# Three edits in a two-layer cross-attention kernel: seven block products for the FFN's down product, the fold of the sums of squares between the halves of the V projection, the index constants in a step of their own

## The chip, the cores and the metric

The kernel runs on one core of a Trainium2 chip. A core has a matrix engine (TensorE, PE in the profile, with its weight loads shown apart as PEld), a vector engine (VectorE, DVE), a scalar engine (ScalarE, ACT), a general engine (GpSimd, POOL) and a queue that issues the transfers (SyncE, SP). Each engine works through its own queue in order; semaphores tie the queues together. The metric is the device time of one execution in microseconds (us), as the median of several executions. Apart from these, one execution is recorded by the hardware profiler; the views of the profile are of that one.

## The reference: what is computed

2048 tokens of width 512 pass through four blocks, each with a residual: cross attention, a gated feed-forward network, a second cross attention, and a small memory network. In short:

```python
x = x + xattn0(layernorm(x), ctx)      # 32 query heads, 8 key/value heads of 128, rotary positions
w_gu = dequant(qweight_gu, qzeros_gu, scales_gu, g_idx_gu)      # 4-bit weights, 512 x 2752
gate, up = split(layernorm(x) @ w_gu)                           # 1376 columns each
w_d = dequant(qweight_down, qzeros_down, scales_down, g_idx_down)
x = x + (silu(gate) * up) @ w_d                                 # the down product, 1376 -> 512
q, k = rmsnorm(h @ wq, q_w), rmsnorm(ctx @ wk, k_w)             # second attention, h = layernorm(x)
x = x + (softmax(q @ k.T / sqrt(128) + mask) @ v) @ wo
x = x + memory_network(layernorm(x))
```

`dequant` is `scale[g] * (nibble(w) - (nibble(z)[g] + 1))`, where `g` is the group that an index list gives for each row. The rms norm of the second attention divides each head's vector by the root of its mean square, so it needs sums of squares over the 128 elements of a head.

## The kernel before

The tokens are worked on in four chunks of 512 (`c`). In an attention layer a step is one pair of a key/value head `g` (0 to 7) and a chunk `c` (0 to 3), 32 steps per layer. The feed-forward network has 24 steps: six groups of hidden columns (five of 256, the last of 96) by four chunks. Everything is 32-bit floating point; a matmul of the program shows as two instructions in the trace.

**Block products.** Most large products are done by a scheme that needs seven block products instead of eight for a product of 2 by 2 blocks. `left_sums` (L166 to L169, on POOL) forms four sums of the left operand's blocks, `right_sums` (L174 to L177, on POOL) four of the right operand's; a tile of seven blocks (`NBLK`) holds the four originals and the sums. `product` (L186) multiplies one pair of blocks, given by the table `PRODUCTS`, into one bank of PSUM, the memory that PE writes to. Two forms use it. `quarters` makes the four quarters of a result from seven products, for the query projection (P from xnT and wq) and for the gate and up product (P from xnT and wgu); ACT copies intermediate results out (h, L209). The attention's output product (O from oT and wo) adds its seven products into the residual `x_sb` with VectorE (L592): five adds cover one quarter (512 elements per partition), two cover a half (1024). Product 6 accumulates onto the bank of product 1 and product 7 onto that of product 6, each after the add that reads the bank.

**An attention step.** `run` writes the steps one after another, with the next step's projections amid the present step's work: the rest of the previous output product (4, 6, 5, 3, 7) with the pieces of the present softmax between, the next step's key projection (pk, L339) and query projection (P), the present step's product of probabilities and values (po, L566), which ACT copies to oT (L574), the next step's V projection (pv, L369), the first two output products, and the next step's scores (S, L470).

**The fold in the second attention.** VectorE reduces the squares of keys and queries to partial sums (kpart L357, part L425). `norms` adds them up across partitions with small matmuls against a constant (pm, L445 and L452), VectorE adds the epsilon (qs, L458), POOL raises the result to the power -1/2 (qr, L229 in `rsqrt`), and VectorE spreads the query factors over the partitions (rb, L278). The scores are multiplied by both factors (L504), POOL adds the mask (L514), VectorE takes maxima (r2x, L525). `run` calls `norms` for the next step after the values product, then `left_sums(oT)`, then the V projection.

**The feed-forward network.** A step makes hT = silu(gate) * up for one group and chunk (`ffn_up`; VectorE adds L878, POOL products L885). The down product of the previous step follows (`ffn_down`, L896): per 128 tokens two matmuls, 128 x 512, and one add into the residual (L903). In steps 1 to 3 of a group the next group's weights are unpacked (`nibbles`, L836) and dequantised (L831, L832), with small matmuls (pgz, pdz, L850) that gather scales and zero points by one-hot rows.

**The index constants.** `ffn_constants` is a generator: each of its pieces is emitted in one step of the first attention, from step (1,0) on, behind an add of the output product. The first piece makes the index columns pidx (L727 to L730) and also the first 512 columns of scales (casts L744 and L746, products L745). Later pieces take further scales, then zero points, then the one-hot rows.

A tile framework gives each engine its queue. Within what the program's order and the buffers allow, it chooses the order of instructions on each queue by their priorities, so an edit to the order of emission can shift instructions on several engines.

Of the kernel before, what the change touches and what calls it, by code (L numbers as in the profile page):

```python
# [44 lines left out]
def tile_xattn_ffn_2_layers(ctx: ExitStack, tc: tile.TileContext, a: dict, out: bass.AP):  # L45
# [133 lines left out]
    def product(which, ps, left, right, widths=(P, P), first=True):  # L179


        l, r = PRODUCTS[which]
        pv = ps.rearrange("p (m n) -> p m n", m=2)
        for m, w in enumerate(widths):
            for k in range(2):
                nc.tensor.matmul(  # L186
                    pv[0:w, m, :],
                    left[:, l, k, m * P : m * P + w],
                    right[:, r, k, :],
                    start=(first and m == 0 and k == 0),  # L190
                    stop=(k == 1),
                    skip_group_check=True,
                )

    def quarters(n, left, right, done, widths=(P, P)):


        size = (slice(0, widths[0]), slice(0, len(widths) * HC))

        def mul(which, ps=None):  # L200
            new = ps is None
            if new:
                ps = mm_tile(f"P{which}_{n}")
            product(which, ps, left, right, widths, first=new)
            return ps

        def copy(which, ps):
            t = half_tile(f"h{which}_{n}")
            nc.scalar.copy(t[size], ps[size])  # L209
            return t  # L210

        x = mul(1)
        p1 = copy(1, x)
        done(0, 0, p1, mul(2))
        mul(6, x)
        u2 = copy(2, x)
        w = mul(5)
        p5 = copy(5, w)
        mul(3, w)
        done(0, 1, u2, w)  # L220
        mul(7, x)
        u3 = copy(3, x)
        done(1, 1, p5, x)
        done(1, 0, u3, mul(4))


    def rsqrt(dst, src):
# [59 lines left out]
    class Attention:  # L287
# [71 lines left out]
            )  # L359
            return kT, part  # L360

        def project_v(self, g, c, ctxT):
            n = f"{self.L}_{g}_{c}"
            wkv = self.wkv[g]
            v = ap_.tile([P, TT, HD], F32, tag="v", name=f"v{n}")
            ps = mm_tile(f"pv{n}")
            for t in range(TT):
                for k in range(KT):
                    nc.tensor.matmul(  # L369
                        ps[:, t * HD : (t + 1) * HD],  # L370
                        ctxT[:, k, t * P : (t + 1) * P],
                        wkv[:, k, 1, :],
                        start=(k == 0),
                        stop=(k == KT - 1),
                    )
            nc.scalar.copy(v.rearrange("p t d -> p (t d)"), ps)
            return v
# [205 lines left out]
            return ps  # L583

        def out_add(self, c, rows, cols, ps, over=None):

            x = x_sb[c].rearrange("p (i t) (j w) -> p i t j w", i=2, j=2)
            dst = x[:, rows] if cols is None else x[:, :, :, cols] if rows is None else x[:, rows, :, cols]
            src = ps.rearrange("p (t w) -> p t w", t=2)
            if over is not None:  # L590
                src = src.unsqueeze(over).to_broadcast(dst.shape)
            self.added = nc.vector.tensor_tensor(dst, dst, src, ALU.add).ins  # L592

        def output_first(self, g, c, oT):

# [39 lines left out]
        def run(self, hooks, joined, after, between=lambda c: None, tail=lambda: None, late={}):  # L635
# [15 lines left out]
            for i, (g, c) in enumerate(steps):  # L651
                more = i + 1 < len(steps)
                if c == NCH - 1 and g + 1 < NKV:
                    self.load_kv(g + 1)
                for hook in hooks.get((g, c), ()):
                    hook()
                ctx_next = ctx_of(i + 2) if i + 2 < len(steps) else None
                if g == NKV - 1 and c > 1:
                    between(c - 2)
                pieces = self.softmax(g, c, st, scales)  # L660

                def middle():
                    if c == NCH - 1 and g + 1 < NKV:
                        with tc.issue_after(self.pooled):
                            left_sums(self.wq[g + 1])

                if before is not None:
                    probs = self.output_rest(*before, pieces, middle)
                    with tc.issue_after(self.added):
                        for hook in late.get((g, c), ()):  # L670
                            hook()
                else:
                    *_, probs = pieces
                if c == 0 and g > 0:
                    self.load_out(g)
                done = before is not None and before[0] == NKV - 1
                if done:
                    joined(before[1])
                if more:
                    kT, kpart = self.project_k(*steps[i + 1], ctxT)  # L680
                    if c == 0:
                        right_sums(self.wo[g])
                    qT, part = self.project_q(*steps[i + 1])
                    if c == NCH - 2 and g + 1 < NKV:
                        self.load_q(g + 1)
                else:
                    tail()
                if done:
                    after(before[1])
                oT = self.values(g, c, v, probs)  # L690
                if more:
                    scales = self.norms(*steps[i + 1], kpart, part)
                self.pooled = left_sums(oT)
                if more:
                    v = self.project_v(*steps[i + 1], ctxT)
                before = self.output_first(g, c, oT)
                if more:
                    st = self.scores(*steps[i + 1], kT, qT)
                ctxT = ctx_next
# [10 lines left out]
    def ffn_constants():  # L710
# [5 lines left out]
        for base, cnt, parts in ((R_GS, NG, 3), (R_GZ, NG, 1), (R_DS, NGD, 3), (R_DZ, NGD, 1)):  # L716
# [11 lines left out]
            nc.vector.tensor_scalar(p2, idx, float(2 * cnt), -1.0, ALU.is_ge, ALU.mult)  # L728
            for p_ in (p1, p2):
                nc.vector.scalar_tensor_tensor(idx, p_, float(cnt), idx, ALU.mult, ALU.add)  # L730
        for base, cnt, name in ((R_GS, NG, "scales_gu"), (R_DS, NGD, "scales_down")):
            rows = slice(base, base + 3 * cnt)
            _, p1, p2 = (pidx[rows, k : k + 1] for k in range(3))
# [33 lines left out]
        for base, cnt, parts, name in (  # L767
# [7 lines left out]
            for at in range(0, total, CH):  # L775
# [11 lines left out]
                    oh[rows, at : at + w], o, pidx[rows, 0:1], None, ALU.is_equal  # L787
                )
                yield
        ffn["sz"], ffn["oh"] = sz, oh  # L790

    groups = [(f, min(FG, INTER - f)) for f in range(0, INTER, FG)]
    wgu, wd = {}, {}
# [17 lines left out]

    def ffn_load_down(i):

        d = (
            q_tile(f"wd{i}")[:, 0:2]
            if i % 2 == 0
            else o_tile(f"wd{i}").rearrange("p b h w -> p b (h w)")[:, 0:2]
        )
        for t, (f, w_) in enumerate(ffn_tiles(i)):
            nc.sync.dma_start(  # L820
                d[0:w_, t, :].bitcast(U32),
                a["qweight_down"][f // 8 : (f + w_) // 8, :]
                .unsqueeze(1)
                .to_broadcast([w_ // 8, 8, D]),
            )
        wd[i] = d

# [12 lines left out]
    def ffn_dequant(i, what=None):  # L840
# [18 lines left out]
        if what in (None, 1):  # L859
            left_sums(w, fw)  # L860
        for t, (f, w_) in enumerate(ffn_tiles(i)) if what in (None, 2) else ():
            nibbles(d[0:w_, t, :], w_)
            pp = [mm_tile(f"pdz{i}_{t}_{side}") for side in range(2)]
            for side, rows in enumerate((slice(R_DS, R_DS + 3 * NGD), slice(R_DZ, R_DZ + NGD))):
                nc.tensor.matmul(
                    pp[side][0:w_, :], oh[rows, f : f + w_], sz[rows, 0:D], start=True, stop=True
                )
            dequant(d[0:w_, t, :], pp[0][0:w_, :], pp[1][0:w_, :])

    def ffn_up(i, c):  # L870
        hT = tmp_tile(f"hT{i}_{c}")
        widths = [w_ for _, w_ in ffn_tiles(i)]
        size = (slice(0, widths[0]), slice(0, len(widths) * HC))

        def quarter(j, half, x, y):

            x, y = x[size], y[size]
            nc.vector.tensor_tensor(x, x, y, ALU.add)  # L878
            h = hT[0 : widths[0], 0 : len(widths), half * HC : (half + 1) * HC]
            xv = x.rearrange("p (t w) -> p t w", w=HC)  # L880
            if j == 0:
                nc.scalar.activation(xv, xv, AF.Silu)
                held[half] = xv
            else:
                nc.gpsimd.tensor_tensor(h, held[half], xv, ALU.mult)  # L885

        held = {}
        quarters(f"{i}_{c}", wgu[i], xnT[c], quarter, widths)
        return hT

    def ffn_down(i, c, hT):
        tiles = ffn_tiles(i)
        for tk in range(TT):
            p = mm_tile(f"pd{i}_{c}_{tk}")
            for t, (f, w_) in enumerate(tiles):
                nc.tensor.matmul(  # L896
                    p,
                    hT[0:w_, t, tk * P : (tk + 1) * P],
                    wd[i][0:w_, t, :],
                    start=(t == 0),  # L900
                    stop=(t == len(tiles) - 1),
                )
            nc.vector.tensor_tensor(x_sb[c][:, tk, :], x_sb[c][:, tk, :], p, ALU.add)  # L903

    def ffn_run(hooks, joined, last):
# [398 lines left out]
```

## Time and profile before

| | us |
|---|---|
| median of 3 executions | 2937.34 (2937.07 to 2941.98) |
| the profiled execution | 2943.32 |
| its span in the profile | 2941.5 |
| first attention, about | 0 to 1206 |
| feed-forward network, about | 1206 to 1677 |
| second attention, about | 1677 to 2860 |
| memory network, to the end | 2860 to 2941.5 |

| engine, busy us | first attention | feed-forward | second attention | end |
|---|---|---|---|---|
| PE | 1155.9 | 470.2 | 1156.1 | 56.7 |
| DVE | 884.4 | 200.0 | 677.2 | 50.5 |
| ACT | 399.4 | 94.5 | 303.1 | 23.2 |
| POOL | 624.9 | 114.4 | 523.9 | 20.7 |

The mean granted clock of PE over the execution was 0.987 of full speed. A row of a timeline reads: start, duration, engine, line, operation, out<-in, shape, number of instructions merged into the row, and in square brackets the idle time before it with what ended it. A row of the waits reads: who waited <- for whom: us in total, times, the longest one. A row of the groups reads: line, engine, operation, out<-in, shapes, count | busy us, mean ns of one | idle time before, releaser.

### The profile page before, as it was taken

Reading aid. Unit: us, or ns where it says so; the run is one execution under the profiler, and the core shown is the slowest. Engines: PE = TensorE matmul, PEld = TensorE weight load, DVE = VectorE, ACT = ScalarE, POOL = GpSimd, SP = SyncE. Lnnn points to the kernel's source line nnn. Section 1 sums busy time; section 2 is a strip of 40 time slices with the busy share of each in tenths; the row PEclk is TensorE's granted clock in tenths of the full one; section 3 lists DMA queues with packets and bytes.
Section 4 is the critical chain, followed back from the end, with each engine's and each line's share of the span. In section 5 each row is a group of like instructions: output and inputs, shape, how many; then the busy total and the mean of one; then the engine's idle time right before and its main releaser. Section 6 shows DMA issues by size and latency. Waiting matters only on the chain.

```text
span 2941.5 us, 40415 instructions
## 1 busy us (share of the span) xinstructions
PE 2838.8 (97%) x16502; PEld 2217.1 (75%) x16502; DVE 1812.1 (62%) x2752; ACT 820.2 (28%) x1397; POOL 1283.9 (44%) x932
## 2 busy tenths in 40 slices
PE   7999999999999999899999999999999999999987
PEld 5878787778887787676666677777777777787765
DVE  7667777777777766544433665555555555555565
ACT  3323333333333333211111222222222222222232
POOL 5544545454545455411222444444445353535432
PEclk9999999999999999899999999999999999999998
DMA  4111111111111111000000102120202020201001
GB/s 159 40 44 44 52 45 51 49 60 51 45 52 44 51 44 58 23 22 22 20 8 17 36 29 67 34 65 30 65 29 65 30 65 29 65 31 64 15 1 58
DMA packets 103807, 130.71 MB, mean 44 GB/s; under 512 B 8725, under 2 KB 65165, under 8 KB 103623
## 3 DMA queue, kind: packets, MB, share of 16 engines
q1 hardware_dynamic: 103047, 127.09, 13.3%
q8 instruction: 130, 2.13, 0.3%
q10 hardware_dynamic: 576, 1.05, 0.1%
q14 instruction: 54, 0.44, 0.1%
HBM read 123.92 MB, written 4.19 MB: 44 GB/s over the span
## 4 chain that ended last, share of the span: by engine, by line
PE 80%; DVE 12%; ACT 3%; issue 2%; POOL 2%; DMA 0%; DVEq 0%; ACTq 0%; POOLq 0%
PE P L186 30%; PE O L186 22%; PE pv L369 8%; PE pk L339 6%; PE pd L896 5%; PE S L470 4%; DVE part L425 2%; PE po L566 2%; DVE x L592 2%; DVE qT L419 1%; ACT q L421 1%; ACT rq L384 1%; DVE S L493 1%; PE pqy L1014 1%; DVE r2x L525 1%
## 5 line engine op out<-in xcount | busy, mean ns | idle before, releaser
L186 PE MATMUL P<-xnT,wq 128*128 128x256 f32 x3584 | 799.2, 382 | 23.4 <-ACT h L209 21.9
L186 PE MATMUL O<-wo,oT 128*128 128x256 f32 x3584 | 803.8, 382 | 4.2 <-ACT oT L574 3.3
L186 PEld LDWEIGHTS P<-xnT,wq 128*128 128x128 f32 x3584 | 678.8, 191 | 159.2 <-issue 39.2
L186 PEld LDWEIGHTS O<-wo,oT 128*128 128x128 f32 x3584 | 671.4, 190 | 118.0 <-issue 22.1
L592 DVE TENSOR_TENSOR x<-x,O 128x512 f32<-128x512 f32 (+1 forms) x448 | 368.5, 823 | 145.6 <-PE O L186 145.1
L546 POOL TENSOR_TENSOR s<-s,ib 128x512 f32<-128x512 f32 x128 | 169.6, 1347 | 489.0 <-DVE ib L278 480.5
L209 ACT COPY h<-P 128x512 f32<-128x512 f32 (+1 forms) x352 | 200.1, 573 | 365.4 <-PE P L186 354.5
L388 POOL TENSOR_TENSOR qT<-h,rq 128x512 f32<-128x512 f32 x128 | 175.4, 1370 | 277.1 <-DVE rq L387 267.2
L186 PE MATMUL P<-xnT,wgu 128*128 128x256 f32 (+1 forms) x1232 | 273.8, 382 | 0.0
L540 ACT ACTIVATE s<-s 128x1024 f32<-128x1024 f32 x64 | 67.7, 1057 | 708.1 <-DVE s L538 708.1
L186 PEld LDWEIGHTS P<-xnT,wgu 128*128 128x128 f32 (+1 forms) x1232 | 228.0, 187 | 47.1 <-issue 7.4
L229 POOL TENSOR_TENSOR qr<-qs,nhalf 128x20 f32<-128x20 f32 x32 | 113.4, 3543 | 335.0 <-DVE qs L458 335.0
L369 PE MATMUL pv<-wkv,ctxT 128*128 128x128 f32 x1984 | 238.0, 278 | 3.0 <-DVE h L401 1.7
L369 PEld LDWEIGHTS pv<-wkv,ctxT 128*128 128x128 f32 x1984 | 226.2, 192 | 14.0 <-issue 8.6
L384 ACT COPY rq<-h 64x512 f32<-64x512 f32 x256 | 157.9, 617 | 245.3 <-DVE h L401 242.9
L339 PE MATMUL pk<-ctxT,wkv 128*128 128x512 f32 x496 | 223.1, 592 | 0.0
L419 DVE TENSOR_TENSOR qT<-h,P 128x512 f32<-128x512 f32 x128 | 83.9, 674 | 170.4 <-PE P L186 170.4
L885 POOL TENSOR_TENSOR hT<-h,h 128x512 f32<-128x512 f32 (+1 forms) x48 | 55.6, 1179 | 283.4 <-DVE h L878 263.7
L339 PEld LDWEIGHTS pk<-ctxT,wkv 128*128 128x128 f32 x496 | 94.1, 190 | 92.9 <-issue 89.9
L896 PE MATMUL pd<-wd,hT 128*128 128x512 f32 (+1 forms) x352 | 155.0, 592 | 0.0
L386 DVE TENSOR_TENSOR h<-h,cosT 128x512 f32<-128x512 f32 x128 | 90.0, 703 | 105.0 <-ACT rq L384 105.0
L878 DVE TENSOR_TENSOR h<-h,P 128x512 f32<-128x512 f32 (+1 forms) x96 | 59.6, 640 | 151.9 <-PE P L186 103.7
(235 smaller groups left out, 3234.4 us busy)
## 6 DMA issues: line engine op xcount, KB each, us to landing
ctxT<-in_ctxT SPq DMA_DIRECT2D x62, 1024.0 KB
wq<-in_L_wq SPq DMA_DIRECT2D x32, 256.0 KB
wo<-in_L_wo SPq DMA_DIRECT2D x32, 256.0 KB
wq<-in_L_wqT SPq DMA_DIRECT2D x32, 256.0 KB
wo<-in_L_woT SPq DMA_DIRECT2D x32, 256.0 KB
wgu<-in_qweight_gu SPq DMA_DIRECT2D x40, 128.0 KB
out<-o SPq DMA_DIRECT2D x16, 256.0 KB
x<-in_x SPq DMA_DIRECT2D x12, 256.0 KB
```

The source lines that it names most:

```text
L186: nc.tensor.matmul(pv[0:w, m, :], left[:, l, k, m * P : m * P + w], right[:, r, k, :], start=(first and m == 0 and k == 0), stop=(k == 1), ...
L209: nc.scalar.copy(t[size], ps[size])
L229: nc.gpsimd.tensor_tensor(dst, src, nhalf[:, : src.shape[-1]], ALU.pow)
L339: nc.tensor.matmul(ps, wkv[:, k, 0, :], ctxT[:, k, :], start=(k == 0), stop=(k == KT - 1))
L369: nc.tensor.matmul(ps[:, t * HD : (t + 1) * HD], ctxT[:, k, t * P : (t + 1) * P], wkv[:, k, 1, :], start=(k == 0), stop=(k == KT - 1),)
L384: nc.scalar.copy(t[lo:hi, 1], src[HD - hi : HD - lo])
L388: nc.gpsimd.tensor_tensor(dst(None), dst(x), dst(t[:, 1]), ALU.add)
L419: nc.vector.tensor_tensor(q, xv, yv, ALU.add)
L470: nc.tensor.matmul(s5[j * KB : (j + 1) * KB, f, e], kT[:, f, e, j], qT[:, f * 4 + j].rearrange("p h q -> p (h q)"), start=True, stop=True,)
L546: nc.gpsimd.tensor_tensor(sv[:, f], sv[:, f], ib[:, f * W : (f + 1) * W].unsqueeze(1).to_broadcast([P, KH, W]), ALU.mult,)
L592: self.added = nc.vector.tensor_tensor(dst, dst, src, ALU.add).ins
L896: nc.tensor.matmul(p, hT[0:w_, t, tk * P : (tk + 1) * P], wd[i][0:w_, t, :], start=(t == 0), stop=(t == len(tiles) - 1),)
```

## The change

Three places change. First, in the five full groups the down product takes the scheme of seven block products: `right_sums` of the down weights after their dequantisation, `left_sums` of hT after its making, then seven products of two matmuls (four instructions) 128 x 256, whose results a new function `join` adds into the residual (the former body of `out_add`). hT and the down weights lie in tiles of seven blocks; for full groups hT takes a buffer of the context tiles. The last group of 96 keeps the old form. Second, `norms` is called between the two halves of the V projection, and `left_sums(oT)` is emitted after the V projection. Third, the index columns end with a `yield` of their own, so the first scales and all later pieces come one step later.

```diff
@@ product
-            for k in range(2):
+            for k in range(left.shape[2]):
...
-                    stop=(k == 1),
+                    stop=(k == left.shape[2] - 1),
@@ new function; out_add now calls it
+    def join(c, rows, cols, ps, over=None):
+
+        x = x_sb[c].rearrange("p (i t) (j w) -> p i t j w", i=2, j=2)
+        dst = x[:, rows] if cols is None else x[:, :, :, cols] if rows is None else x[:, rows, :, cols]
+        src = ps.rearrange("p (t w) -> p t w", t=2)
+        if over is not None:
+            src = src.unsqueeze(over).to_broadcast(dst.shape)
+        return nc.vector.tensor_tensor(dst, dst, src, ALU.add).ins
@@ project_v
-        def project_v(self, g, c, ctxT):
+        def project_v(self, g, c, ctxT, middle=lambda: None):
...
             for t in range(TT):
+                if t == TT // 2:
+                    middle()
                 for k in range(KT):
@@ run
                 oT = self.values(g, c, v, probs)
                 if more:
-                    scales = self.norms(*steps[i + 1], kpart, part)
+                    scales = []
+
+                    def middle():
+                        scales.append(self.norms(*steps[i + 1], kpart, part))
+
+                    v = self.project_v(*steps[i + 1], ctxT, middle)
+                    scales = scales[0]
                 self.pooled = left_sums(oT)
-                if more:
-                    v = self.project_v(*steps[i + 1], ctxT)
@@ ffn_constants
                 nc.vector.scalar_tensor_tensor(idx, p_, float(cnt), idx, ALU.mult, ALU.add)
+        ffn["sz"], ffn["oh"] = sz, oh
+        yield
         for base, cnt, name in ((R_GS, NG, "scales_gu"), (R_DS, NGD, "scales_down")):
...
-        ffn["sz"], ffn["oh"] = sz, oh
@@ ffn_load_down
+        d = home[:, 0 : NBLK * HC].rearrange("p (b k w) -> p b k w", b=NBLK, k=1)
@@ ffn_dequant
+        if what in (None, 2) and fw == FG:
+            right_sums(d)
@@ ffn_up
-        hT = tmp_tile(f"hT{i}_{c}")
+        if len(ffn_tiles(i)) == 2:
+            hT = ctx_tile(f"hT{i}_{c}").rearrange("p a b -> p (a b)")[:, 0 : NBLK * HC]
+        else:
+            hT = tmp_tile(f"hT{i}_{c}").rearrange("p a b -> p (a b)")
+        hT = hT.rearrange("p (b k w) -> p b k w", k=1, w=HC)
...
         quarters(f"{i}_{c}", wgu[i], xnT[c], quarter, widths)
+        if len(widths) == 2:
+            left_sums(hT)
@@ ffn_down
+        if len(tiles) == 2:
+
+            def mul(which, ps=None):
+                new = ps is None
+                if new:
+                    ps = mm_tile(f"D{which}_{i}_{c}")
+                product(which, ps, hT, wd[i], first=new)
+                return ps
+
+            x = mul(1)
+            join(c, 0, 0, x)
+            join(c, 0, 0, mul(2))
+            join(c, 1, 0, mul(4))
+            mul(6, x)
+            join(c, 0, 1, x)
+            join(c, None, 1, mul(5), 1)
+            join(c, 0, 1, mul(3))
+            mul(7, x)
+            join(c, 1, None, x, 2)
+            return
```

## The prediction

> **What bounds the kernel now.** I read the page first (busy shares, groups), then PE's waits, then the timeline of one step of each stage that the change touches.
>
> ```profile
> PE 2838.8 (97%) x16502; PEld 2217.1 (75%) x16502; DVE 1812.1 (62%) x2752; ACT 820.2 (28%) x1397; POOL 1283.9 (44%) x932
> L229 POOL TENSOR_TENSOR qr<-qs,nhalf 128x20 f32<-128x20 f32 x32 | 113.4, 3543 | 335.0 <-DVE qs L458 335.0
> L896 PE MATMUL pd<-wd,hT 128*128 128x512 f32 (+1 forms) x352 | 155.0, 592 | 0.0
> ```
>
> PE is busy for 97%: time is won by giving it less, or lost where it is made to stop. Of its waits, the part concerns these two:
>
> ```profile
> PE P L186 <- ACT h L209: 21.9, 15, 6.2
> PE pm L445 <- DVE part L425: 10.9, 29, 0.6
> ```
>
> The first holds the 6.2 us at the first step with index constants; the second is the fold of layer 1, 29 stops of 0.376. Now a feed-forward step and the gate/up product behind it (start, duration):
>
> ```profile
> 1303.84 7.03 PE L896 MATMUL pd<-wd,hT 128*128 128x512 f32 x16
> 1310.70 12.38 PE L186 MATMUL P<-xnT,wgu 128*128 128x256 f32 x56
> 1322.92 7.03 PE L896 MATMUL pd<-wd,hT 128*128 128x512 f32 x16
> ```
>
> From start to start: 6.86 us for 16 matmuls 512 wide, 0.429 each; 12.22 for 56 matmuls 256 wide, 0.218 each. And a step of layer 1, from the fold on:
>
> ```profile
> 2032.93 2.05 ACT L574 COPY oT<-po 128x512 f32<-128x512 f32 x4 [0.50 <-PE po L566]
> 2033.23 0.27 PE L445 MATMUL pm<-part,fold 128*32 128x16 f32 x7 [0.37 <-DVE part L425]
> ...
> 2033.91 3.54 POOL L229 TENSOR_TENSOR qr<-qs,nhalf 128x20 f32<-128x20 f32 x1 [12.11 <-DVE qs L458]
> 2037.16 3.62 PE L186 MATMUL O<-wo,oT 128*128 128x256 f32 x16
> ...
> 2037.42 1.27 POOL L166 TENSOR_TENSOR oT<-oT 128x512 f32<-128x512 f32 x1
> 2037.49 0.71 DVE L278 STREAM_TRANSPOSE rb<-qr 128x512 f32<-128x512 f32 x1 [3.66 <-POOL qr L229]
> 2039.10 0.69 DVE L592 TENSOR_TENSOR x<-x,O 128x512 f32<-128x512 f32 x1 [0.90 <-PE O L186]
> ...
> 2041.22 1.29 POOL L169 TENSOR_TENSOR oT<-oT 128x512 f32<-128x512 f32 x1
> 2042.58 8.90 PE L186 MATMUL O<-wo,oT 128*128 128x256 f32 x40
> ```
>
> PE runs fold, V projection, output products 1 and 2, scores, then 4, 6, 5, 3, 7, without a stop behind the fold. POOL's power (3.54 us) starts as soon as the fold is done, and its four left sums follow (5.09 from 2037.42 to the end of L169). DVE is in order: rb waits for the power, and the adds of products 1 and 2 stand behind rb.
>
> **Down product.** In 20 of 24 steps 16 matmuls of 0.429 (6.86) become 28 matmuls 256 wide. Price by the nearest rows: 0.2182 (the 56 above), 0.2185 (40 output products in 8.74, 2042.58 to 2051.32), upper bound 803.8/3584 = 0.224 (the group, with its slow stretches). At 0.2185: 6.12, so 0.74 a step, 14.8 in all (11.6 at 0.224).
> The Trainium skill, page "TensorE: Matmul & The Clock Gate", section "Back-to-back issue gap", speaks against this: sustained it gives about 81 ns at 128 columns and 131 at 512, so halving the width does not halve the time. An estimate from it, 98 ns at 256 by a straight line, makes 28 halves 1.31 times 16 wholes: 2.1 us lost per step, 42 in all. The two rows above disagree (0.218 against 0.429), and the measurement decides.
>
> Beside PE: DVE's 4 adds become 5 of 512 and 2 of 1024 elements, by the output products' adds (0.69 alone, 0.65 in a row, 1.21 for 1024). Laid behind the seven products of 0.875, from the first at 0: adds end at 1.76, 2.64, 3.52, 4.40, 5.80 (the double one), 6.5, 7.8. Product 7 needs the fourth at 5.25: it has it. The next matmuls take banks at 6.12 (of products 4, 2, 5: free by 5.8), 6.8 (needs 6.5) and 8.5 (needs 7.8): no stop. Only in the four steps c = 3 do three nibble operations of 0.49 (L836), which wait for weights, stand among these adds; the sixth then ends near 7.2, 0.5 late. That is 2 us in all, and up to 3 each, 12, if the weights are later. Should the adds fall behind in all 15 steps with dequantisation by 0.7, 11 are lost: that end stays for the range. Four left sums of hT (POOL, 1.27 each, one step ahead of their use) and four right sums per group lie under 18.4 us steps in which POOL works 114 of 471 us; without that cover a step would wait up to 5.1. hT now lives in context buffers, so two context loads of layer 1 go behind one set of its wq loads on SP's queue, 30 to 40 us before their use: nothing. **Down: -14.8 + 2 = -12.8** (-15 to 0).
>
> **Fold amid the V projection.** 31 of 32 folds move back by 8 of 16 matmuls, 1.84 us of PE (half of the 3.67 from 2033.49 to 2037.16). The stop of 0.376 goes, since the last partial sum (DVE, to 2033.17) is there: -10.9 in all, no more. What is late next? The power is now behind the four left sums in POOL's queue: in 31 steps the changed program issues L166 to L169 first, then L229, because the fold comes late while oT is ready with its last copy at 2034.98. From there, by these rows (times less 2000):
> left sums 35.06 to 40.15; power to 43.68 (before: 37.45); rb 43.72 to 44.43; add of product 1 to 45.01. PE, 0.37 earlier, ends product 4 at 43.96, and product 6 accumulates into product 1's bank: it waits for that add until 45.07, **1.11**. Behind it DVE: add of 2, four score products from 45.5, add of 4, maxima at +3.55 as before, add of product 6 to 50.91; product 7 needs that bank: it could start at 50.31 and starts at 50.97, **0.66**. Then PE runs freely: the probabilities' last products end some 4 us later, near 62 for 57.96, and are needed at 68; DVE reaches the queries' adds of the next step as PE has their inputs, 1.4 later too.
> So 31 x 1.77 = 54.9 lost, 10.9 won: **+44.0**. Ends: if only the first stop comes, 31 x 1.11 - 10.9 = +23.5; if L169 takes its longest time in the trace (2.26 for 1.29) in every step, 31 x 2.74 - 10.9 = +74; if the order on POOL costs nothing, -10.9. I take the middle, which follows the most frequent durations. The output products' left sums lose nothing: they end at 40.15 and were ready at 42.51.
>
> **Index constants.** At step (1,0) 16 tiny DVE operations on pidx and the first piece of scales stand in DVE's queue from 195.0 on, and delay the key rotation to 205.84 and with it the copies on ACT:
>
> ```profile
> 205.84 0.67 DVE L386 TENSOR_TENSOR rk<-pk,cosT 128x512 f32<-128x512 f32 x1
> ...
> 209.99 8.02 PE L186 MATMUL P<-xnT,wq 128*128 128x256 f32 x24 [6.18 <-ACT h L209]
> ```
>
> Without the piece (casts 1.21, 0.41, 0.40, two products 0.74: 3.5) DVE is free about 3.4 earlier; the stop falls to some 2.8. The 24 matmuls behind it took 8.02 instead of 5.24 (24 x 0.2185), with the clock granted at 0.50 up to 214. A stop of 2.74 at 1151 was followed by 24 matmuls in 6.83, one of 0.63 at 320 by 24 in 5.42: so another 1.4 comes back. The piece itself goes one step on, and the last of all into a step that had none; pieces elsewhere are followed by stops of 0.3 to 1.8, 6 in all, which move with them (±2). Its DMAs (three small ones) and those of all later pieces pass one step's context, wo and wq loads on SP's queue; those have a step's slack. **-4.8** (-6.8 to -1.4).
>
> **Sum:** -12.8 + 44.0 - 4.8 = +26.4. The profiled execution (2943.3; span 2941.5) would become 2969.7. The median is 6.0 below that execution, so 2937.3 + 26.4 = **2963.7**.
>
> **Rivals.**
> 1. *The order on POOL costs nothing* (the other side): if the power gets ahead of the left sums after all, or the sums take half their time when DVE is idle, product 6 does not wait. It decides at the end of the power: up to 42.6 (1.11 before my 43.68) the first stop is gone, at 41.9 the second. For it: the power and the sums need only 8.6 of 36 us. Against: in-order queues (rb waits 3.66 for the power in the row above), and the sums' duration varies little (1.26 to 1.29 mostly). -12.8 - 10.9 - 4.8 = -28.5: 2908.8.
> 2. *The stops cost clock too.* Two stops a step, 1.77 in all, behind each other; a stop of 2.74 took 1.6 from the next 24 matmuls, stops of up to 1.8 nothing seen. If each step lost 1.5 that way: +46, 3010.
> The same page, section "What's actually happening", has the clock fall only after an idle window of about 3.4 us; the slower matmuls behind 2.74 us of stop stand against that. By the page this rival gives nothing.
> 3. *The down product brings nothing*: seven adds (5.9 us of DVE) behind 6.1 us of products, with dequantisation between, take the gain back: +12.8, 2976.5. For it: DVE loses its slack. Against: it is busy 200 of 471 us there. That the product does not do what it says would give the same.
>
> **How the numbers follow.** Forecast 0.70, its own range from 2940 (first stop only, -15, -6.2: +2.3) to 2988 (stops of 2.2, -5, -2.8: +50); rival 1 0.12; rival 2 0.08; rival 3 0.10. A range of 2940 to 2990 leaves out rival 1, most of rival 2 and a little of the forecast: 2 in 10. A measurement can tell 0.2%, 5.9 us: 2931.5 to 2943.2 counts as the same. Faster: rival 1 and a scrap of the forecast, 0.13; same: the forecast's low end, 0.05; slower 0.82.
>
> **What would show it.** Right: down products near 6.1 us with no wait of PE behind them; PE's wait for part (L425) gone; in layer 1 L229 starting after L169, rb some 6 us later, and two new waits of the output products for the add at L592's counterpart, near 1.1 and 0.7 us, some 60 in all; the wait of P for h at (1,0) near 2.8. Wrong: L229 ahead of L166, no new wait there; gate/up products or pgz waiting for the adds of D; a granted clock under 0.98 in layer 1.

## The result and the profile after

The changed kernel takes 2986.28 us (median of 5 runs, 2984.58 to 2987.8) against 2938.85 us before: a ratio of 1.0157, with a 95% interval of 1.0143 to 1.0171. It is 47 us slower. The direction is the one forecast (+26.4), and the time lies inside the range; the size is short by 21 us, and the runs below say in which terms. The kernel before took 2938.85 us beside the changed kernel and 2940.50 us beside e1 to e4 below, so a difference between the changed kernel and one of these runs is good to about 2 us.

The page of the changed kernel, its busy shares and the group of the output products:

```profile
PE 2845.4 (95%) x16742; PEld 2262.8 (76%) x16742; DVE 1861.8 (62%) x2812; ACT 820.1 (27%) x1397; POOL 1354.1 (45%) x1032
...
L186 PE MATMUL O<-wo,oT 128*128 128x256 f32 x3584 | 819.0, 383 | 44.8 <-DVE x L233 38.2
```

The same group before:

```profile
L186 PE MATMUL O<-wo,oT 128*128 128x256 f32 x3584 | 803.8, 382 | 4.2 <-ACT oT L574 3.3 <-POOL oT L167 0.9
```

PE works as long as before (2845 for 2839 us; that is a mean over gains and losses, since clock and pipelining enter it), but the span grew by 41 us, and the output products, which had stood idle for 4.2 us in the whole execution, now have 44.8. The waits of PE (who waited, for whom, total us, times, longest):

```profile
PE O L186 <- DVE x L233: 38.2, 58, 0.8
PE P L186 <- ACT h L209: 20.8, 14, 3.8
...
PE xtc L265 <- DVE xnc L260: 3.9, 2, 2.5
...
PE P L186 <- DVE x L233: 2.5, 4, 0.8
...
PE O L186 <- DVE fc L1026: 2.3, 1, 2.3
```

The first row did not exist before; the fold's wait (pm for part, 10.9) is gone. The rows for xtc and fc are new as well, and no step of the prediction had them. The one for P behind an add is the feed-forward stage. A step of the second attention, in the timeline (the same stretch as the prediction shows of before):

```profile
2044.47 1.27 POOL L169 TENSOR_TENSOR oT<-oT 128x512 f32<-128x512 f32 x1
...
2045.70 3.54 POOL L238 TENSOR_TENSOR qr<-qs,nhalf 128x20 f32<-128x20 f32 x1
2046.08 1.93 PE L481 MATMUL S<-qT,kT 128*32 128x256 f32 x32
2047.95 1.99 PE L186 MATMUL O<-wo,oT 128*128 128x256 f32 x8
2049.28 0.71 DVE L287 STREAM_TRANSPOSE rb<-qr 128x512 f32<-128x512 f32 x1 [8.29 <-POOL qr L238]
2049.91 1.44 DVE L233 TENSOR_TENSOR x<-x,O 128x512 f32<-128x512 f32 x2
2050.71 5.42 PE L186 MATMUL O<-wo,oT 128*128 128x256 f32 x24 [0.76 <-DVE x L233]
...
2056.68 1.99 PE L186 MATMUL O<-wo,oT 128*128 128x256 f32 x8 [0.56 <-DVE x L233]
...
2058.51 3.60 PE L348 MATMUL pk<-ctxT,wkv 128*128 128x512 f32 x8
```

The power starts when the last left sum ends, rb follows it, the two adds follow rb, and PE stops twice: before product 6 (2050.71) and before product 7 (2056.68). From product 4 to the next key projection it takes 10.56 us (2047.95 to 2058.51) where the kernel before took 8.74 (from 2042.58, shown with the prediction, to the row below): 1.82 us per step. The idle times listed add up to only 1.32. The ends of matmuls are modelled, so a stop is better read from start to start: product 4 takes 1.75 us (8 instructions at 0.2185), which leaves 1.01 for the first stop, and 24 instructions take 5.24, which leaves 0.73 for the second.

```profile
2051.32 3.60 PE L339 MATMUL pk<-ctxT,wkv 128*128 128x512 f32 x8
```

### The profile page after: what moved, and what is told of

It reads as the page before. It is cut to its first block, busy times and chain, and to the rows that moved or that the text cites. A ratio compares the mean times of both kernels' runs of the same rounds, so it can differ in the third digit from the quotient of the medians.

```text
span 2982.8 us, 41223 instructions
## 1 busy us (share of the span) xinstructions
PE 2845.4 (95%) x16742; PEld 2262.8 (76%) x16742; DVE 1861.8 (62%) x2812; ACT 820.1 (27%) x1397; POOL 1354.1 (45%) x1032
## 4 chain that ended last, share of the span: by engine, by line
PE 67%; DVE 14%; POOL 12%; ACT 4%; issue 2%; DMA 1%; SPq 0%; DVEq 0%; ACTq 0%; POOLq 0%
PE P L186 31%; PE O L186 13%; PE pk L348 6%; PE pv L380 4%; PE po L577 4%; POOL qr L238 4%; DVE x L233 4%; PE D L186 3%; POOL s L525 2%; ACT oT L585 2%; PE S L481 2%; DVE r2x L536 2%; POOL oT L166 1%; POOL oT L167 1%; POOL oT L168 1%
## 5 line engine op out<-in xcount | busy, mean ns | idle before, releaser
L186 PE MATMUL O<-wo,oT 128*128 128x256 f32 x3584 | 819.0, 383 | 44.8 <-DVE x L233 38.2
L380 PE MATMUL pv<-wkv,ctxT 128*128 128x128 f32 x1984 | 246.2, 280 | 3.0 <-DVE h L412 1.7
L166 POOL TENSOR_TENSOR oT<-oT 128x512 f32<-128x512 f32 x64 | 81.0, 1266 | 347.1 <-ACT oT L585 347.1
L287 DVE STREAM_TRANSPOSE rb<-qr 128x512 f32<-128x512 f32 x32 | 22.8, 711 | 257.9 <-POOL qr L238 257.9
```

What stands on the lines that cost most here:

```text
L166: tt(b[4], b[2], b[3], ALU.add)
L186: nc.tensor.matmul(pv[0:w, m, :], left[:, l, k, m * P : m * P + w], right[:, r, k, :], start=(first and m == 0 and k == 0), stop=(k == lef ...
L380: nc.tensor.matmul(ps[:, t * HD : (t + 1) * HD], ctxT[:, k, t * P : (t + 1) * P], wkv[:, k, 1, :], start=(k == 0), stop=(k == KT - 1),)
```

## The experiments

The theory, Q: the loss is made by POOL's queue, in which the power now stands behind four left sums. The rival, V: cutting the V projection by the fold costs PE itself. The other two parts were run alone.

**1. The fold back in its place (e1).**

```diff
@@ run, against the changed kernel
+                    scales = self.norms(*steps[i + 1], kpart, part)
                 self.pooled = left_sums(oT)
+                    v = self.project_v(*steps[i + 1], ctxT)
```

> The changed kernel with the fold again ahead of the V projection and the power ahead of the left sums; the down product and the index step stay. Theory Q (the loss comes from the power standing behind four left sums on POOL) and theory V (the loss comes from the fold cutting the V projection on PE) both expect the gains of the other two parts alone, as the trace of the changed kernel shows them: -2.4 us up to the first output product of the last step of layer 0, -10.5 us in the feed-forward stage, so some 12.8 us under before, near 2926. Well above 2930 would mean that the other two parts also cost something in layer 1.

Measured: 2932.28 us, ratio to before 0.9973 (0.9962 to 0.9985). The fold part costs 2986.3 - 2932.3 = 54 us, and what remains is a gain of 8, not 12.8: a first sign that one of the other two parts brings less.

**2. Only POOL's order changed (e2).** In the second attention the left sums wait for the power. The fold stays amid the V projection, and the queues of the other engines hold the same instructions in the same order as in the changed kernel.

```diff
-                self.pooled = left_sums(oT)
+                if more and self.L == 1:
+                    with tc.issue_after(self.power):
+                        self.pooled = left_sums(oT)
+                else:
+                    self.pooled = left_sums(oT)
```

> The changed kernel with nothing changed but POOL's queue: in layer 1 the four left sums of oT wait for the power, so the power runs first; the fold stays amid the V projection, and PE, DVE, ACT and SP have the very same order as in the changed kernel. Theory Q: the waits of the output products for the adds behind rb (38 us) go, the wait for part stays away, 0.25 us a step is won: near 2926 - 8 = 2918. Theory V: the order on POOL is beside the point, it stays above 2970. If the sums, now late, hold up products 6, 5 or 3, a new wait for oT (L167 or L169) appears.

Measured: 2925.71 us, ratio 0.9956 (0.9941 to 0.9971). The order on one queue is worth 60.6 us. Its timeline:

```profile
2057.53 0.18 DVE L469 TENSOR_SCALAR qs<-pm 128x20 f32<-128x20 f32 x1 [2.02 <-PE pm L463]
2057.79 3.54 POOL L238 TENSOR_TENSOR qr<-qs,nhalf 128x20 f32<-128x20 f32 x1 [13.13 <-DVE qs L469]
...
2061.30 1.27 POOL L166 TENSOR_TENSOR oT<-oT 128x512 f32<-128x512 f32 x1
2061.37 0.71 DVE L287 STREAM_TRANSPOSE rb<-qr 128x512 f32<-128x512 f32 x1 [3.65 <-POOL qr L238]
...
2064.67 8.90 PE L186 MATMUL O<-wo,oT 128*128 128x256 f32 x40
```

The power starts with the fold, and the five last output products run in one stretch of 40 instructions. The left sums, now late, hold nothing up: one step earlier the last of them ends at 2030.47, 1.71 us behind the start of product 4 (2028.76), and the products run on. The step lasts 35.91 us (power to power, 2021.88 to 2057.79), 36.16 in the first experiment (2021.60 to 2057.76): the moved fold by itself gains 0.25 us a step. Theory V falls.

**3. A smaller and a larger dose (e3, e4).** In e3 three sums stand ahead of the power and one behind it; in e4 the fourth sum is formed twice, so five stand ahead. The queues of the other engines are again those of the changed kernel.

```diff
@@ e3, in run for layer 1
-                self.pooled = left_sums(oT)
+                    for s_ in range(3):
+                        left_sum(oT, s_)
+                    with tc.issue_after(self.power):
+                        self.pooled = left_sum(oT, 3)
@@ e4, in run for layer 1; the power and rb are emitted behind the fifth sum
                 self.pooled = left_sums(oT)
+                    fifth = nc.gpsimd.tensor_tensor(b[6], b[1], b[5], ALU.subtract).ins
+                    with tc.issue_after(fifth):
+                        scales = scales()
```

> A dose between: three left sums ahead of the power, the fourth behind it, else the changed kernel. Theory Q: power, rb and adds come 1.27 us earlier; the first stop (0.76 us in the changed kernel's trace) is gone, the second (0.56) shrinks to 0.1 to 0.2, since PE arrives some 0.8 to 0.9 earlier and the add 1.27: 2918 + 31 x 0.15, near 2923. If the loss went with the number of sums ahead without a threshold, a quarter of it would go: near 2969. Theory V: above 2970.

Measured: 2948.21 us, ratio 1.0025 (1.0015 to 1.0034). That is 22.5 us above e2: neither the 5 that I had expected nor the 45 of a proportional loss. A step of e3:

```profile
2038.71 7.17 PE L197 MATMUL O<-wo,oT 128*128 128x256 f32 x32
...
2046.22 1.99 PE L197 MATMUL O<-wo,oT 128*128 128x256 f32 x8 [0.34 <-DVE x L244]
```

The first stop is gone: products 4, 6, 5, 3 run through. Before product 7, PE stops for 0.51 us (2046.22 - 2038.71 - 7.0 for 32 instructions). The rule that I had applied was right and its input wrong: I had subtracted from the listed idle time (0.56). From the stop read start to start it comes out: 0.73, less the 1.27 by which the add comes earlier, plus the 1.01 by which PE does, is 0.47. From power to power the 26 regular steps of e3 last 36.52 us against 35.91 in e2, which makes 16 of the 22.5 us; the rest lies in the irregular steps.

> A larger dose: the fourth left sum is formed twice, so five stand ahead of the power, else the changed kernel. Theory Q: there is no slack left, so the add of product 1 comes 1.27 us later in each of 31 steps and PE with it: +39 us on the changed kernel, near 3025; the first stop near 2.0 us, the second as before. Theory V: no more than a few us over 2986. If stops of 2 us also cost clock, clearly over 3030.

Measured: 3043.06 us, ratio 1.035 (1.0335 to 1.0365), 57 us above the changed kernel where 39 was expected. The clock is the main reason, as its timeline and then its windows show (the last columns of a window: granted clock, DMA share, GB/s):

```profile
2069.64 8.83 PE L186 MATMUL O<-wo,oT 128*128 128x256 f32 x32 [2.12 <-DVE x L233]
```

```profile
2065.00:2069.60 4.60, 2.53 (x20) 1.56 (x12) 1.28 (x2) 0.00 (x0) 3.18 (x1) 1.00 0.00 0
2069.60:2072.00 2.40, 2.35 (x8) 2.02 (x9) 2.40 (x6) 0.00 (x0) 0.78 (x1) 0.71 0.00 0
2072.00:2074.00 2.00, 2.00 (x7) 1.56 (x6) 0.71 (x2) 0.00 (x0) 1.71 (x2) 0.50 0.00 0
2074.00:2076.00 2.00, 2.00 (x11) 1.77 (x10) 1.97 (x4) 0.00 (x0) 0.00 (x0) 0.99 0.00 0
```

Behind a stop of 2.1 us the clock drops to 0.50 for some 3 us, and 32 instructions take 8.83 us instead of 7.17. Not every step is hit. A step behind a stop of the same length, where the clock stayed at 1.00 and the second stop came as before:

```profile
1990.63 5.42 PE L186 MATMUL O<-wo,oT 128*128 128x256 f32 x24 [2.12 <-DVE x L233]
1996.61 1.99 PE L186 MATMUL O<-wo,oT 128*128 128x256 f32 x8 [0.56 <-DVE x L233]
```

From power to power, 10 of the 26 regular steps of e4 last about 39.1 us, near the 1.3 expected above the 37.74 of the changed kernel, and 16 last about 39.95. Those 16 times 0.85 make 14 of the 18 us above the expectation. So the loss follows the dose: 2926, 2948, 2986, 3043 us with none, three, four and five sums ahead of the power. The fourth sum costs about what it lasts (38 us, 1.22 a step), the fifth more, because its stops cost clock. No run had one or two ahead; an estimate from the 0.61 us a step that three cost (36.52 against 35.91), which is less than the 1.27 of one sum, is that two cost nothing.

**4. Each part alone, on the kernel before (e5, e6, e7).** The diffs are the three parts of the change.

> The kernel before with the second part alone: the fold amid the V projection and the left sums emitted behind it, so that POOL runs them ahead of the power. Theory Q, with the fold part's price as the difference of the changed kernel and the one with the fold back (2986.3 - 2932.3 = 54.0): +54, near 2994. Rival S (the loss needs the down product too, through DVE or POOL work pushed into layer 1): clearly less, +20 or below.

Measured: 2995.56 us, ratio 1.0191 (1.0177 to 1.0205), +54.9. The down product is not needed for the loss. The new waits for xtc and fc are here too, in the waits of e5:

```profile
PE O L186 <- DVE x L594: 38.4, 57, 1.1
...
PE xtc L256 <- DVE xnc L251: 3.9, 2, 2.5
PE O L186 <- DVE fc L989: 2.3, 1, 2.3
```

> The kernel before with the third part alone. My step: the stop at (1,0) falls from 6.2 to some 2.8 and half of the slow stretch behind it goes, -4.8. What the changed kernel's trace says: the stop there is 3.6, the 24 matmuls behind it still take 8.02, -2.5, and other steps give a part of that back: between -2.5 and +1 us, within what can be told from nothing.

Measured: 2942.45 us against 2940.65, ratio 1.0004 (0.9995 to 1.0013): nothing. The timeline shows that the stop was not taken away but moved:

```profile
488.35 0.32 SPq L755 DMA_DIRECT2D qz<-in_qzeros_gu  x1
488.72 0.88 SPq L327 DMA_DIRECT2D wo<-in_L_wo  x2
...
491.78 0.81 DVE L758 TENSOR_SCALAR zi<-qz 4x344 uint32<-4x344 uint32 x1 [2.04 <-DMA qz<-in_qzeros_gu]
...
501.72 8.49 PE L186 MATMUL P<-xnT,wq 128*128 128x256 f32 x24 [4.04 <-ACT h L209]
```

Read by the starts of the values products, the step with the index columns shrinks from 44.40 to 41.00 us. But the first piece of zero points is now in step (3,0), where its load is issued between those of the output weights. DVE stands for 2.04 us on it, the key rotation behind it is late, and PE stops for 4.04 us and then runs at a reduced clock: that step grows from 36.22 to 42.73.

Both figures hold for one execution. In every profiled execution that has this piece and its load in step (3,0) DVE waits for the load, but not equally long: the changed kernel, e1, e2, e4 and e9 stop for 2.83 us there, and the step lasts 40.16; e3 stops for 4.03, and it lasts 41.36. At (1,0) the stop is 3.64 to 3.67 us in the changed kernel, e1 to e4, e6 and e11. The 24 matmuls behind it take 7.13 us in all of these but the changed kernel's profiled execution, where they take 8.02, so that its step lasts 41.86 and the others 40.98 to 41.00. The row of the changed kernel, then that of e6:

```profile
206.38 8.02 PE L186 MATMUL P<-xnT,wq 128*128 128x256 f32 x24 [3.64 <-ACT h L209]
207.17 7.13 PE L186 MATMUL P<-xnT,wq 128*128 128x256 f32 x24 [3.67 <-ACT h L209]
```

> The kernel before with the first part alone. My step: -12.8. From the stages of the changed kernel: -10.5. If the down product really takes more of layer 1 (its hT in the context buffers, two late context loads), less than 8 remains.

Measured: 2930.31 us, ratio 0.9965 (0.9953 to 0.9978), -10.3. The three parts alone add up to 54.9 + 1.8 - 10.3 = +46.4, which is the whole change within its interval (+42 to +50).

**5. The index part with early loads of zero points (e11).** The two loads are issued one piece earlier, with the last piece of scales.

```diff
+            if name == "scales_down":
+                qz = m2_tile("qz").bitcast(U32)
+                zi = m2_tile("zi").bitcast(U32)
+                for zb, zn, zname in ((R_GZ, NG, "qzeros_gu"), (R_DZ, NGD, "qzeros_down")):
+                    nc.sync.dma_start(qz[zb : zb + zn, 0 : a[zname].shape[1]], a[zname])
...
-            nc.sync.dma_start(qz[rows, 0:w], a[name])
```

> The index part alone, again with the two loads of zero points one piece earlier. Theory L (the part won 3.4 us at (1,0) and lost 6.5 at (3,0), because the loads of zero points slid among the output weights' loads): step (3,0) goes back from 42.7 to some 37 and the whole is 3 to 5 us under the kernel before, near 2936. Theory N (narrow operations and right sums of that step do it): no change, near 2942.

Measured: 2938.48 us against 2941.6, ratio 0.9989 (0.9980 to 0.9998). Step (3,0) is back to 37.21 us:

```profile
489.04 0.33 DVE L760 TENSOR_SCALAR zi<-qz 4x344 uint32<-4x344 uint32 x1
...
498.52 5.45 PE L186 MATMUL P<-xnT,wq 128*128 128x256 f32 x24 [1.56 <-ACT h L209]
```

DVE no longer waits for the load, PE's stop is 1.56, and the 24 instructions behind it take 5.45: theory L holds. The kernel before stops for 0.58 us in this step, which has narrow operations of zero points there too; of the 0.98 more, one cast accounts, which takes 1.90 us in e11 (489.40) and 0.93 before (494.21). Why it is slower isn't shown. The row of before:

```profile
502.36 5.45 PE L186 MATMUL P<-xnT,wq 128*128 128x256 f32 x24 [0.58 <-ACT h L209]
```

**6. A version that beats both (e9, e10).** To e2, e9 adds two things: the nibble operations of the next gate and up weights are held behind the last add of the down product in which they stood, and the index columns are made in four steps, (0,1) to (1,0). e10 adds the early loads of zero points.

```diff
+            with tc.issue_after(mem["join"]) if "join" in mem else ExitStack():
                 nibbles(wk, P)
...
+            if base == R_DZ:
+                ffn["sz"], ffn["oh"] = sz, oh
+            yield
...
-        late={(g, c): [lambda: next(pieces, None)] for g in range(1, NKV - 1) for c in range(NCH)},
+        late={(g, c): [lambda: next(pieces, None)] for g in range(NKV - 1) for c in range(NCH) if g + c},
```

> A version meant to beat both: the changed kernel with the left sums behind the power, the nibble operations of the next gate/up weights held behind the last add of the down product that they stood in, and the index columns made in four steps, (0,1) to (1,0), instead of one. From the version with the sums behind the power (2925.7): the waits of PE for adds in the feed-forward stage (4.8 us in the changed kernel) go, unless the unpacked weights come late in their place; the 3.6 us stop at (1,0) falls under 1.8 and the clock stays up there, 3.6 + 2.8 - 1 = 5 us. Near 2916; not under 2922 if the nibbles only trade one wait for another.

Measured: 2917.94 us, ratio 0.9920 (0.9907 to 0.9934). In the feed-forward stage, the changed kernel's timeline shows how the nibbles (L849) held up the adds:

```profile
1283.59 0.49 DVE L849 TENSOR_SCALAR wgu<-wgu,sh 128x512 uint32<-128x512 uint32 x1
...
1284.80 0.83 DVE L849 TENSOR_SCALAR wgu<-wgu,sh 128x512 uint32<-128x512 uint32 x1
...
1286.68 0.47 DVE L849 TENSOR_SCALAR wgu<-wgu,sh 128x512 uint32<-128x512 uint32 x1
1287.08 1.80 DVE L233 TENSOR_TENSOR x<-x,D 128x512 f32<-128x512 f32 x2
```

There the next product started 1.64 us after the small pdz matmuls (1286.16 to 1287.80); in the same step of e9 it is 0.54, and PE waits for no add in that stage. The step with the index columns takes 35.46 us; only the one with the first zero points remains, at 40.16.

> The version with four index steps, and the two loads of zero points issued one piece earlier, with the last piece of scales, so that they do not stand among the output weights' loads of step (3,0). If the late load is what makes the new stop of 4 us there (the trace of the index part alone shows DVE waiting 2.04 us for it), that step takes 36 to 38 us instead of 40.2: near 2915. If the narrow operations and POOL's sums of that step make it anyway, 2918 as before.

Measured: 2912.38 us, ratio 0.9902 (0.9887 to 0.9917): 1% under the kernel before, with all three parts of the change in it. Step (3,0) lasts 37.18 us, 3.0 less than in e9; the other 2.6 us between the two medians are not traced to a step.

## Why the prediction was right in kind and short in size

Of the 21 us that the forecast is short, the parts measured alone account for 20: the fold part for 10.9 (+54.9 for +44.0), the index part for 6.6 (+1.8 for -4.8) and the down product for 2.5 (-10.3 for -12.8). All three were taken too favourably.

- **The fold and POOL's order.** The mechanism is shown: e2 removes the loss by POOL's order alone, e3 and e4 move it with the dose. The two stops were put at 1.11 and 0.66 (1.77 a step); measured from start to start they are 1.01 and 0.73, in all 1.82 with the tail. This term was right: 54.9 predicted, 56.4 for 31 steps. That the left sums lose nothing also came true: in the changed kernel they end at 2045.74, before product 4 begins at 2047.95.
- **The gain of the moved fold was too large.** "-10.9 in all, no more" took the whole listed wait of pm as won. A step gains 0.25 us, 31 steps 7.8, and e1 against e2 gives 6.6. From the values product's start to the output product it is 6.06 us (2074.21 to 2080.27) where before it was 6.31 (2030.85 to 2037.16). The cut gives a part of the 0.376 back: the two halves of the V projection take 1.98 and 1.88 us from start to start (2076.15 to 2078.13, 2078.39 to 2080.27) where the whole took 3.67.
- **Two waits were missed.** xtc (3.9) and fc (2.3), both in steps where other work stands in DVE's queue (the normalisation of the last chunk, the memory network's constants) and is now late as well: 6.2 us. In e2 1.4 of the wait for xtc is still there, so that much belongs to the moved fold and not to POOL's order. I had laid out one regular step and multiplied it by 31. With these corrections, 44.0 + 1.5 + 3.1 + 6.2 = 54.8, and e5 measures 54.9 with an interval of 52 to 60; that the two agree to 0.1 is luck, since the irregular steps lose other amounts than the regular ones.
- **The down product.** The price of a matmul was near: the 28 take 6.14 us up to the pgz matmuls behind them, where the 16 of before took 6.96 (1322.92, shown with the prediction, to 1329.89), so 0.82 is won per step and not 0.74, 16.4 in all. The stop by the nibbles in the four steps c = 3 was right in place and too small: the next product starts 1.6 to 2.0 us after the pdz matmuls where before it was 0.53, so 1.1 to 1.5 each and not 0.5, since one nibble operation took 0.83 and the adds behind it slid further. In e7 the four stops come to 4.9 us: -16.4 + 4.9 = -11.5, and e7 measures -10.3 (-13.8 to -6.5). The two errors, 1.6 too little won and 2.9 too little lost, partly cancel. Before, then the changed kernel:

```profile
1329.89 0.60 PE L850 MATMUL pgz<-szoh 12*128 12x512 bf16 x4
```

```profile
1261.02 6.21 PE L186 MATMUL D<-wd,hT 128*128 128x256 f32 x28
1267.16 0.60 PE L863 MATMUL pgz<-szoh 12*128 12x512 bf16 x4
...
1362.53 1.11 PE L879 MATMUL pdz<-szoh 30*128 30x512 bf16 x4
1364.48 12.49 PE L186 MATMUL P<-xnT,wgu 128*128 128x256 f32 x56 [0.84 <-DVE x L233]
```

- **The index constants: the step that failed.** "Its DMAs and those of all later pieces pass one step's context, wo and wq loads on SP's queue; those have a step's slack." The slack of the loads that were passed does not matter; the piece's own load needs to be early, and it had no slack: DVE waited 2.04 us for it in e6, and e11 takes that wait away. My ±2 for "pieces elsewhere" came from averaging over steps that are alike, and (3,0) is not: it has the output weights' loads and POOL's right sums. At (1,0) I had 3.4 for the stop and 1.4 for the clock; e6 gives 2.5 (6.18 to 3.67) and 0.9 (8.02 to 7.13), in all 3.4 (44.40 to 41.00). The stop shrank less because DVE reached the key rotation only 2.3 us sooner: 8.43 us from the transpose of ib (194.06 to 202.49 in the changed kernel) for 10.70 before (195.14 to 205.84). At (3,0) e6 loses 6.5. In the changed kernel's profiled execution the two steps last 41.86 and 40.16, which comes to a loss of 1.4; there the clock gave nothing back (8.02 behind a stop of 3.64).
- **The rivals.** Rival 1 (POOL's order costs nothing) was false of this kernel, and e2 is what it would have been: 2925.7, not 2908.8, by the same overrated gains. Rival 2 (stops cost clock) does not hold at stops of 0.7 and 1.0 us (the changed kernel's granted clock is 1.00 from 2046 to 2060), and does at 2.1, one left sum further, in part of the steps. Rival 3 took place for three tenths of the gain of the down product (4.9 of 16.4), by nibbles and not by the adds alone.

## What to carry to other kernels

An edit that moves one operation of a queue later lets whatever is ready pass it; read the new order of every queue and lay the step out with it before counting what the edit saves. Here 5 us of POOL work that nobody waited for, passing an operation of 3.5 us that everybody waited for, cost 60.6 us where the moved fold by itself wins 6.6 (e1 against e2), and a hint to the scheduler brought it back. Then look at the irregular steps one by one: where a generator's pieces are shifted, each piece takes its loads into a new neighbourhood on the transfer queue.

## What the hardware showed that was not expected

A stop of PE listed as 2.12 us can halve the granted clock for 3.4 us (0.50 in the window above); a stop of 1.56 us in e11 was followed by 24 matmuls in 5.45 us, and those of 0.7 to 1.0 us by none slower. Which stops count can be read from the record of the granted clock in e4's trace. Its low stretches last 3.41 us or a whole multiple of that (the last one runs into the end of the program), and they begin whole multiples of 3.413 us apart, as on a fixed grid. The output products of the second attention have 28 stops listed at 2.07 to 2.12 us. Of these, 17 began between 0.1 us before and 1.4 us after a point of that grid, so that nearly all of the stop lay between two points, and the clock was 0.50 from the next point on. The other 11 began 2.3 to 3.2 us after a point and ran across the next one, and the clock stayed at 1.00. So in this execution the place of a stop on the grid decided, and not its length alone; that fits the steps (1,0) and (3,0), whose times differ between executions. The page "TensorE: Matmul & The Clock Gate" of the Trainium skill, section "What's actually happening", has the clock fall after an idle window of about 3.4 us; here 2.1 us of standing still within such a stretch were enough, and the measurement decides.

The second point is one of reading: idle time listed for PE was 1.32 us in a step that lost 1.82 from start to start, so small repeated stops are to be priced from starts.
